# All products of an attention step in quarters of the TensorE array, with sums of 64 keys

## The chip, the cores and the metric

The kernel runs on one core of one Trainium2 chip. The metric is device time in microseconds, the median of several runs. Besides these runs one execution was taken by the hardware profiler; all rows of profiles here come from such an execution.

## The reference

A transformer block with modulated normalization over x of 32 batches x 256 tokens x 128 features, all in float32:

- `mod = silu(c) @ wmod` gives six rows for each batch; two of them are gates, kept at least 0.25 from zero.
- `h = layernorm(x) * (1 + ca) + sa`, then a root-mean-square norm of `h`, then queries, keys and values of 16 heads with 64 features each.
- `scores = q k^T`, without a scale, -inf where the key is later than the query. The softmax runs over the *query* axis (`axis=-2`): each key's column is normalized over the queries that see it.
- `z = attn @ v`, projected by `W_o`; `x = x + ga * (...)`.
- A second normalization and a mixture of 32 experts (4 groups of 8, two groups and six experts for a token, 64 inner features), with a shared expert and one anchor expert of a token: `x = x + gb * (routed + shared + 0.1 * anchor)`.

## The kernel before, in words

The tokens are cut into 16 chunks of 512 tokens (two batches). Attention takes 8 steps for a chunk, one for each pair of heads, so there are 128 steps; a step `s` belongs to chunk `s // 8`. What a step does is written out in the loop over `s`, and each engine runs its instructions in the order in which this loop issues them. No planner moves them.

In step `s` TensorE computes the scores of the pair `s`, the weighted sums of the pair `s - 2`, the queries and keys of the pair `s + 2`, the output product of the pair `s - 3`, and a quarter of the values of half a chunk. Keys stand on the partitions, since the softmax runs over queries.

- `score_products` (L528, products at L542) uses 64x64 quarters of the array: 64 keys of one head against the queries that see them, four at a time, into four banks of PSUM, one for each batch and head. `e` of a batch and head is a tile of 384 columns: 256 for the first 128 keys and 128 for the others.
- `lowest` (L566) on VectorE adds the mask and takes the minimum of each key's row; `exponential` (L576) on ScalarE takes the exponential and its sum. Queries carry a minus sign for this. `inverse_sums` (L584) and, on GpSimd, `scaled_values` (L595) scale the values by the inverse sums.
- `weighted_sums` (L613) multiplies 128 keys at a time: scaled values as weights of 128 rows and 64 columns, against 256 or 128 queries. `heads_out` (L624) copies the result to SBUF.
- Query, key, value and output products (`in_halves`, L492) run as two column halves of 128 rows by 64 columns. Their results leave PSUM by VectorE (values L504, queries L514) and ScalarE (keys L524). The products take turns on two banks of `ps_mm`; the sums have a bank of their own, the outputs another.

Around the steps lies work of whole chunks, cut into portions. A table gives each portion a step, counted from the chunk's first, and a place in that step (TOP, PROD, MID or END): loads of x and of modulation rows (`load_x`, `load_mod1`, `load_mods`), the first normalization of chunks to come, mostly on GpSimd, the gate and the sum of the attention's output (`rest_gate`, `rest_sum`), the second normalization, and the router with the sending of token rows to lists of experts. Each normalized chunk is turned through DRAM: `through_dram` (L422) writes it and reads it back in four blocked loads, all on SyncE's queue, and VectorE transposes 32x32 blocks (`norm1_turn`, `norm2_turn`). SyncE's queue holds nearly all loads and stores, in program order: 69 writes of blank rows too, three a step from step 0, and the weights of the expert stage, all of them in step 9 (`late_loads`). A buffer that is used again makes its DMA wait: `mb2`, loaded by `load_mods` in step 7 of a chunk, has one buffer, which `norm2_modulate` (L406, on GpSimd) of the chunk before frees.

After the 128 steps and a short run-out comes the expert stage over lists of 512 rows; the change touches only the names of its PSUM banks.

## Time and profile before

| | |
|---|---|
| median of 3 runs | 1357.53 us (1355.21 to 1361.33) |
| the profiled execution | 1363.71 us |
| span of its instructions | 1361.6 us |
| granted TensorE clock, mean | 0.988 |
| TensorE busy | 1309.9 us, 96% of the span |
| VectorE busy | 1035.6 us, 76% |
| ScalarE busy | 866.4 us, 64% |
| GpSimd busy | 759.4 us, 56% |

A span runs from the program's first instruction to its last. PE is TensorE's matmuls and PEld its weight loads, DVE VectorE, ACT ScalarE, POOL GpSimd, SP SyncE; SPq, POOLq are their queues. L613 is line 613 of the kernel. A float32 matmul appears as two passes, so a product of two halves counts four times. In a row with a bar, busy time and the mean of one instruction stand ahead of the idle time of the engine just before such instructions and what ended it. In a timeline the columns are the start and the length in microseconds, the engine, the line, the operation, output and inputs, and the count; in a list of waits they are the total, the number and the longest.

### The profile page before, as it was taken

How to read it: one execution, taken by the hardware profiler on the slowest of the kernel's cores; microseconds unless marked ns; L12 is line 12 of the kernel's file. 1: busy time of each engine (PE TensorE's matmuls, PEld its weight loads, DVE VectorE, ACT ScalarE, POOL GpSimd, SP SyncE). 2: the span in 40 equal slices, each digit the busy share in tenths (PEclk: the TensorE clock that was granted, in tenths of full speed). 3: DMA queues.
4: the chain of work that ended last, by engine and by line, in shares of the span. 5: the costliest groups of instructions: out<-in, count | busy, mean ns of one | idle time of the engine just before them, and what ended most of it. 6: DMA issues, size and time to landing. Idle time of an engine off the chain costs nothing. (4 is left out here: it accounts for less than half of the span.)

```text
span 1361.6 us, 37937 instructions
## 1 busy us (share of the span) xinstructions
PE 1309.9 (96%) x12491; PEld 812.7 (60%) x12491; DVE 1035.6 (76%) x4270; ACT 866.4 (64%) x2883; POOL 759.4 (56%) x1291
## 2 busy tenths in 40 slices
PE   6999899999999999999999997999999999999996
PEld 2555566666666666566566665466666666666664
DVE  5656688888888889889889776666855557888776
ACT  3868687778778777777777876444444544445451
POOL 2636368678669669669669557445332324434342
PEclk8999999999999999999999999999999999999998
DMA  5765821321321221221221212665555556777752
GB/s 159 232 203 200 275 62 32 77 65 37 78 66 40 68 66 40 68 66 40 68 66 40 52 42 55 148 152 130 147 139 127 140 145 183 191 190 191 197 166 70
DMA packets 270702, 153.58 MB, mean 113 GB/s; under 512 B 171014, under 2 KB 234759, under 8 KB 270508
## 3 DMA queue, kind: packets, MB, share of 16 engines
q1 hardware_dynamic: 258908, 129.70, 37.0%
q0 software_dynamic: 10624, 20.40, 4.3%
q8 instruction: 101, 1.65, 0.5%
q10 hardware_dynamic: 976, 1.06, 0.3%
q14 instruction: 93, 0.76, 0.2%
HBM read 91.27 MB, written 60.61 MB: 112 GB/s over the span
## 5 line engine op out<-in xcount | busy, mean ns | idle before, releaser
L576 ACT ACTIVATE e<-e,mn 128x256 f32<-128x256 f32 (+1 forms) x1024 | 453.0, 445 | 186.5 <-DVE mn L566 185.7
L566 DVE CUSTOM_DVE_ANT_0 e<-psc,mask 128x256 f32<-128x256 f32 (+1 forms) x1024 | 305.3, 344 | 7.4 <-ACT th L701 5.1
L1307 POOL DMA_INDIRECT y_d<-y,iy x140 | 140.5, 1003 | 283.1 <-ACT y L1304 247.0
L595 POOL TENSOR_TENSOR vs<-v,rc 128x256 f32<-128x256 f32 x256 | 151.6, 614 | 206.2 <-DVE rc L584 177.0
L1273 DVE TENSOR_TENSOR a<-a,pu 128x512 f32<-128x512 f32 (+2 forms) x185 | 121.5, 657 | 132.6 <-PE pu L1268 126.4
L542 PEld LDWEIGHTS psc<-q,k 64*64 64x64 f32 x4096 | 144.6, 133 | 108.2 <-issue 102.0
L1272 ACT ACTIVATE a<-pg 128x512 f32<-128x512 f32 (+2 forms) x185 | 106.2, 574 | 159.9 <-PE pg L1268 157.1
L613 PE MATMUL pav<-e,vs 128*64 128x256 f32 (+1 forms) x2048 | 195.2, 333 | 6.5 <-POOL vs L595 6.5
L576 ACT ACTIVATION_READ_ACCUMULATOR e<-e,mn 128x1 f32 x1024 | 192.9, 188 | 0.0
L1296 PEld LDWEIGHTS py<-wd_sb,a 128*128 128x128 f32 x1120 | 148.1, 193 | 70.1 <-issue 52.6
L1268 PE MATMUL pg<-h,wg 128*128 128x512 f32 (+2 forms) x370 | 182.5, 575 | 0.0
L1268 PE MATMUL pu<-h,wu 128*128 128x512 f32 (+2 forms) x370 | 181.9, 574 | 0.0
L542 PE MATMUL psc<-q,k 64*64 64x256 f32 (+3 forms) x4096 | 168.7, 303 | 0.0
L492 PEld LDWEIGHTS po<-wo_sb,z 128*64 128x64 f32 x2048 | 123.0, 140 | 70.9 <-issue 67.1
L613 PEld LDWEIGHTS pav<-e,vs 128*64 128x64 f32 x2048 | 127.1, 137 | 53.3 <-POOL vs L595 7.1
L881 POOL DMA_INDIRECT rows_d<-rows,ix x128 | 133.9, 1046 | 39.4 <-issue 33.9
L1296 PE MATMUL py<-wd_sb,a 128*128 x1120 | 150.8, 277 | 2.2 <-DVE a L1274 2.1
L492 PE MATMUL pk<-n_t,wqkv_sb 128*64 128x512 f32 x512 | 133.5, 600 | 3.1 <-DVE v L504 3.1
L492 PE MATMUL pv<-wqkv_sb,n_t 128*64 128x512 f32 x512 | 134.0, 604 | 2.2 <-DVE q L514 2.0
L492 PE MATMUL po<-wo_sb,z 128*64 128x128 f32 x2048 | 136.0, 276 | 0.0
L492 PE MATMUL pq<-n_t,wqkv_sb 128*64 128x512 f32 x512 | 133.6, 600 | 0.7 <-ACT n_t L326 0.7
L504 DVE TENSOR_TENSOR v<-pv,bv_sb 128x512 f32<-128x512 f32 x128 | 87.6, 684 | 58.2 <-PE pv L492 57.5
(240 smaller groups left out, 1798.7 us busy)
## 6 DMA issues: line engine op xcount, KB each, us to landing
rows_d<-blank SPq DMA_DIRECT2D x69, 366.0 KB
bt<-cd SPq DMA_DIRECT2D x70, 256.0 KB
rh<-rows_d SPq DMA_DIRECT2D x140, 64.0 KB
wgr<-in_w_gate_dram SPq DMA_DIRECT2D x35, 256.0 KB
wur<-in_w_up_dram SPq DMA_DIRECT2D x35, 256.0 KB
mb<-mod_dram SPq DMA_DIRECT2D x31, 256.0 KB
hb_ln<-hd_ln SPq DMA_DIRECT2D x124, 64.0 KB
s<-y_d SPq DMA_DIRECT2D x30, 256.0 KB
```

The costliest lines, as they stand in the source:

```text
L492: nc.tensor.matmul(ps[to], a[:, r], b, start=start, stop=stop)
L542: nc.tensor.matmul(pb[h][half * DH : (half + 1) * DH, n // 2 * P + n * DH : n // 2 * P + S,], k[r, o + n * DH : o + (n + 1) * DH], q[r, o ...
L566: nc.vector.tensor_tensor_reduce(e[:, cols], ps[:, cols], mask[:, cols], 1.0, 3e38, ALU.add, ALU.min, mn[:, b, kb, h : h + 1],)
L576: nc.scalar.activation(e[:, cols], e[:, cols], AF.Exp, bias=mn[:, b, kb, h : h + 1], scale=-1.0, accum_out=sm[:, b, kb, h : h + 1],)
L595: nc.gpsimd.tensor_tensor(vs[:, 2 * b : 2 * b + 2], vt[:, 2 * b : 2 * b + 2, col : col + P].rearrange("p k (h d) -> p k h d", h=2), rc[:, ...
L613: nc.tensor.matmul(pav[h * DH : (h + 1) * DH, o + kb * P : o + S], vs[:, 2 * b + kb, h, :], e[:, 0 : 2 * P] if kb == 0 else e[:, 2 * P : 3 ...
L881: sent = nc.gpsimd.indirect_dma_start(out=rows_d[:, :], out_offset=bass.IndirectOffsetOnAxis(ap=ix[:, k, i : i + 1], axis=0), in_=rows[:, ...
L1268: nc.tensor.matmul(ps[:, cols], t[key][k], t["h"][:, cols], start=True, stop=True)
L1272: nc.scalar.activation(a[:, cols], pg[:, cols], AF.Silu)
L1273: nc.vector.tensor_mul(a[:, cols], a[:, cols], pu[:, cols])
L1296: nc.tensor.matmul(t["py"][:, i, :], a[:, i * P : (i + 1) * P], w, start=k == 0 and i == part.start, stop=k == KU and i == part.stop - 1,)
L1307: sent = nc.gpsimd.indirect_dma_start(out=y_d[:, :], out_offset=bass.IndirectOffsetOnAxis(ap=ix[:, i : i + 1], axis=0), in_=y[:, i, :], in ...
```

## The change

All products of steps 3 to 123 are made as 64x64 quarters of the array (`step_in_quarters`). A product that adds 128 rows becomes two row halves, each of two column halves. The two row halves of one product add to the same bank, so they don't run at once: beside the first half of one product runs the second half of another, on another bank. Where a second half could reach a bank while the first is still adding, `done` puts a semaphore instruction into SyncE's queue that waits for the first, and the second waits for that; there are six of these in a step.

The weighted sums are made of 64 keys at a time, against the queries that see any of them (256, 192, 128, 64 columns, from the same tiles `e`).

A step's order on TensorE becomes: scores; first row half of some sums beside the second half of the values of the step before and one output block; queries, first half, beside three output blocks; keys, first half, beside the other sums; queries, second half, beside output blocks, first half; keys, second half, beside values, first half; then, in two steps of a chunk, the router's products (a new place LAST), each row half into a bank of its own, added by VectorE at TOP of the next step.

The sums' own bank goes; sums, queries, keys and values take turns on three banks. Evictions are issued later than their products: keys at the top of the next step, values after the next step's first reductions, queries after the step's last ones. Portions of the table move from TOP to PROD. The way through DRAM is split into a write and, one step later, the loads (`norm1_back`, `norm2_back`). The late weights are loaded one a step from step 17.

```diff
-        ps_mm = actx.enter_context(tc.tile_pool(name="ps_mm", bufs=2, space=PSUM))
-        ps_av = actx.enter_context(tc.tile_pool(name="ps_av", bufs=1, space=PSUM))
+        ps_mm = actx.enter_context(tc.tile_pool(name="ps_mm", bufs=1, space=PSUM))
         ps_wo = actx.enter_context(tc.tile_pool(name="ps_wo", bufs=1, space=PSUM))
+        turns_mm = [0]
+        bank_of = {}
+        def mm_bank(name):
+            turns_mm[0] += 1
+            bank_of[name] = f"mm{turns_mm[0] % 3}"
+            return ps_mm.tile([P, CH], F32, tag=bank_of[name], name=name)
...
-        def through_dram(src, tag, name):
+        def to_dram(src, name):
             hd = hdp.tile([CH, D], F32, tag="hd", name=f"hd_{name}")
             nc.sync.dma_start(out=hd.rearrange("(i p) d -> p i d", p=P), in_=src)
+            return hd
+        def from_dram(hd, tag, name):
             hb = ln.tile([P, CH // BLK, BLK], F32, tag=tag, name=f"hb_{name}")
             load_blocks(hb, hd)
             return hb.rearrange("p x r -> p (x r)")
...
+        def part_of(n):
+            return slice(n * DH, (n + 1) * DH)
+        def wait_for(made, first):
+            tc.add_manual_dep(
+                made.ins, first.ins.name,
+                mybir.DependencyInfo(mybir.DependencyClass.Sync, mybir.DependencyReason.DATA),
+                reason="both halves of the rows add to one bank",
+            )
+        def done(made):
+            seen = nc.sync.nop()
+            wait_for(seen, made)
+            return seen
+        def quarters(ps, r, a, b, start, stop, exchanged=False, behind=None):
+            for h in range(2):
+                made = nc.tensor.matmul(
+                    ps[part_of(1 - h if exchanged else h)], a[part_of(r), part_of(h)],
+                    b[part_of(r)], start=start, stop=stop,
+                )
+                if h == 0 and behind is not None:
+                    wait_for(made, behind)
+            return made
+        def sums_of_quarter(s, pav, b, n, start, stop, behind=None):
+            r = (0, 1, 1, 0)[n]
+            at = n // 2 * P + n * DH
+            for h in range(2):
+                made = nc.tensor.matmul(
+                    pav[part_of(h), b * S + n * DH : (b + 1) * S],
+                    step_of["vs", s][part_of(r), 2 * b + n // 2, h, :],
+                    step_of["e", s][b][h][part_of(r), at : n // 2 * P + S],
+                    start=start, stop=stop,
+                )
+                if h == 0 and behind is not None:
+                    wait_for(made, behind)
+            return made
+        def step_in_quarters(s):
+            w, o = s - LAG, s - LAG - 1
+            c, t = divmod(s + 2, NP)
+            co, to = divmod(o, NP)
+            h2, i = s // HALF + 1, s % HALF
+            cv, j = divmod(h2, 2)
+            n = chunk[c]["n"]
+            nv = chunk[cv]["n"][:, i * P : (i + 1) * P]
+            if i == 0:
+                step_of["v", h2] = vp.tile([P, NT, CH], F32, tag="vt", name=f"v_{cv}_{j}")
+            z = step_of.pop(("z", o))
+            qw, kw = (wqkv_sb[:, k, t * P : (t + 1) * P] for k in range(2))
+            vw = wqkv_sb[:, 2, j * CH : (j + 1) * CH]
+            def output_part(r, k, behind=None):
+                return quarters(
+                    chunk[co]["po"][:, k, :], r, z[:, k * P : (k + 1) * P], wo_sb[:, to, :],
+                    start=to == 0 and r == 1 and k == 0,
+                    stop=to == NP - 1 and r == 0 and k == NT - 1, behind=behind,
+                )
+            if to == 0:
+                chunk[co]["po"] = ps_wo.tile([P, NT, D], F32, tag="po", name=f"po_{co}")
+            pav = mm_bank(f"pav_{s}")
+            sums_of_quarter(w, pav, 0, 0, True, False)
+            rest_of_values()
+            sums_of_quarter(w, pav, 0, 3, False, False)
+            sums_of_quarter(w, pav, 1, 0, False, False)
+            output_part(1, 0, behind=later.pop("po", None))
+            sums = done(sums_of_quarter(w, pav, 1, 3, False, False))
+            pq = mm_bank(f"pq_{s}")
+            queries = quarters(pq, 0, qw, n, True, False)
+            for x in range(1, NT):
+                made = output_part(1, x)
+            step_of["pav", w] = pav
+            sums_of_quarter(w, pav, 0, 1, False, False, behind=sums)
+            pk = mm_bank(f"pk_{s}")
+            before_ = done(queries), done(made)
+            keys = done(quarters(pk, 0, kw, n, True, False))
+            sums_of_quarter(w, pav, 0, 2, False, False)
+            sums_of_quarter(w, pav, 1, 1, False, False)
+            sums_of_quarter(w, pav, 1, 2, False, True)
+            step_of.pop(("vs", w)), step_of.pop(("e", w))
+            heads_out(w)
+            quarters(pq, 1, qw, n, False, True, behind=before_[0])
+            for x in range(NT):
+                made = output_part(0, x, behind=None if x else before_[1])
+            later["po"] = done(made)
+            q, k = (qk.tile([P, CH], F32, tag=x, name=f"{x}_{s + 2}") for x in "qk")
+            step_of["q", s + 2], step_of["k", s + 2] = q, k
+            later["q"] = lambda: nc.vector.tensor_scalar(
+                q, pq, -1.0, negbq[:, t : t + 1], ALU.mult, ALU.add
+            )
+            quarters(pk, 1, kw, n, False, True, behind=keys)
+            later["k"] = lambda: nc.scalar.activation(
+                k, pk, AF.Identity, bias=bqk_sb[:, 1, t : t + 1]
+            )
+            pv = mm_bank(f"pv_{s}")
+            values_ = done(quarters(pv, 0, nv, vw, True, False, exchanged=i % 2 == 1))
+            def rest():
+                quarters(pv, 1, nv, vw, False, True, exchanged=i % 2 == 1, behind=values_)
+                later["v"] = lambda: nc.vector.tensor_add(
+                    step_of["v", h2][:, i, :], pv, bv_sb[:, j * CH : (j + 1) * CH]
+                )
+            later["pv"] = rest
+        later = {}
+        def rest_of_values():
+            later.pop("pv", lambda: None)()
+        def evict(name):
+            later.pop(name, lambda: None)()
...
-            chunk[c]["hb2"] = through_dram(chunk[c]["rows"][:, :, 0:D], "xhln2", f"ln2_{c}")
+            chunk[c]["hd2"] = to_dram(chunk[c]["rows"][:, :, 0:D], f"ln2_{c}")
+        def norm2_back(c):
+            chunk[c]["hb2"] = from_dram(chunk[c].pop("hd2"), "xhln2", f"ln2_{c}")
...
+        def spares(columns):
+            return [score_banks[1][r][:, 3 * P : 3 * P + columns] for r in range(2)]
+        def logits_in_quarters(c):
+            h2 = h2_all[c]
+            pl = spares(NT * E)
+            for i in range(NT):
+                for r in range(2):
+                    quarters(
+                        pl[r][:, i * E : (i + 1) * E], r, h2[:, i * P : (i + 1) * P], gw_sb,
+                        True, True,
+                    )
+            chunk[c]["pl"] = pl
+        def both(out_, ps):
+            nc.vector.tensor_copy(out_, ps[0])
+            nc.vector.tensor_add(out_, out_, ps[1])
+        def logits_tanh(c):
+            x, th = t_([NT, E], "lg", c), t_([NT, E], "th", c)
+            both(x.rearrange("p i e -> p (i e)"), chunk[c].pop("pl"))
+            nc.scalar.activation(th, x, AF.Tanh, scale=0.5)
             chunk[c]["th"] = th
...
-        TOP, PROD, MID, END = range(4)
-        NORM1 = 11
+        TOP, PROD, MID, END, LAST = range(5)
+        NORM1 = 12
         table = [
             (-15, END, load_x),
             (-15, END, load_mod1),
@@ -909,31 +1092,33 @@
             (-9, END, lambda c: norm1_squares(c, 1)),
             (-8, END, norm1_scale),
             (-7, END, norm1_send),
+            (-6, END, norm1_back),
             (-4, TOP, norm1_turn),
             (7, END, load_mods),
             (9, END, rest_bias),
             (11, TOP, rest_gate),
             (12, MID, rest_sum),
             (13, MID, norm2_moments),
-            (14, TOP, norm2_aggregate),
+            (14, PROD, norm2_aggregate),
             (14, END, norm2_normalize),
             (15, END, norm2_modulate),
             (16, END, norm2_send),
-            (19, TOP, norm2_turn),
+            (17, END, norm2_back),
+            (19, PROD, norm2_turn),
             (19, PROD, route_logits),
             (20, MID, route_sigmoid),
-            (21, TOP, route_pairs),
+            (21, PROD, route_pairs),
             (21, MID, lambda c: route_merge(c, 2)),
             (22, MID, lambda c: route_merge(c, 1)),
             (22, END, route_groups),
-            (23, TOP, route_mask),
+            (23, PROD, route_mask),
             (23, END, route_counts),
             (23, MID, route_top),
-            (24, TOP, lambda c: route_marks(c, 6)),
+            (24, PROD, lambda c: route_marks(c, 6)),
             (24, PROD, route_ranks),
             (24, MID, lambda c: route_marks(c, 1)),
-            (25, TOP, route_weights),
-            (26, TOP, route_place),
+            (25, PROD, route_weights),
+            (26, PROD, route_place),
             (26, END, route_write),
             *(
...
+        QUARTERS = range(LAG + 1, NS - HALF)
+        in_quarters = {
+            route_logits: ((19, LAST, logits_in_quarters), (20, TOP, logits_tanh)),
+            route_ranks: ((24, LAST, ranks_in_quarters), (25, TOP, ranks_sum)),
+        }
+        def portions_of(c):
+            for at, where, portion in table[0 if c else NORM1 :]:
+                if portion in in_quarters and c * NP + at in QUARTERS:
+                    yield from in_quarters[portion]
+                else:
+                    yield at, where, portion
...
+        late = late_loads()
         for s in range(NS + LAG + 1):
-            if s == NP + 1:
-                late_loads()
+            if s > 2 * NP:
+                next(late, None)
             ahead = s + 2 < NS
             deal(s, TOP)
+            evict("k")
             if s < NS:
                 score_products(s)
                 for h in range(2):
@@ -1130,6 +1331,24 @@
             if 1 <= s <= NS:
                 inverse_sums(s - 1)
                 scaled_values(s - 1)
+            if s in QUARTERS:
+                step_in_quarters(s)
+                evict("v")
+                deal(s, PROD)
+                for h in range(2):
+                    lowest(s, 1, h)
+                    exponential(s, 1, h)
+                evict("q")
+                if s + 1 not in QUARTERS:
+                    rest_of_values()
+                    evict("v")
+                deal(s, MID)
+                deal(s, END)
+                deal(s, LAST)
+                for i in blanks[s * 3 : s * 3 + 3]:
+                    write_blank(i)
+                step_of.pop("spare", None)
+                continue
```

## The prediction

> **What bounds the kernel now.** I read the page's busy shares first, then busy time by stage, then TensorE's timeline over one step, then the waits of the SyncE queue, then GpSimd's timeline over one chunk.
>
> ```profile
> PE 1309.9 (96%) x12491; PEld 812.7 (60%) x12491; DVE 1035.6 (76%) x4270; ACT 866.4 (64%) x2883; POOL 759.4 (56%) x1291
> ```
>
> ```profile
> 43.30:178.49 135.19, 127.34 (x1539) 77.55 (x1537) 88.24 (x440) 96.89 (x375) 61.24 (x112) 0.97 0.67 222
> 178.49:815.37 636.88, 633.00 (x7991) 391.29 (x7989) 542.67 (x2915) 491.50 (x1947) 462.56 (x857) 1.00 0.22 57
> 403.08:452.95 49.87, 49.87 (x634) 30.97 (x632) 42.92 (x229) 38.85 (x156) 37.74 (x69) 1.00 0.21 54
> ```
>
> The columns are stretch, length, busy PE, weight loads, VectorE, ScalarE, GpSimd, clock, DMA share, GB/s. The first stretch is steps 3 to 22, the second steps 23 to 123: together the 121 steps that the change rewrites, 772.1 us of the span. The third is one chunk of eight steps. In it TensorE has no idle time at a full clock, so TensorE bounds it; but VectorE is busy for 42.9 of 49.9 us, and GpSimd for 37.7. These are next in line.
>
> ```profile
> 399.53 1.03 PE L492 MATMUL pq<-n_t,wqkv_sb 128*64 128x512 f32 x4
> 400.39 1.03 PE L492 MATMUL pk<-n_t,wqkv_sb 128*64 128x512 f32 x4
> 401.25 1.04 PE L492 MATMUL po<-wo_sb,z 128*64 128x128 f32 x16
> 402.12 1.03 PE L492 MATMUL pv<-wqkv_sb,n_t 128*64 128x512 f32 x4
> 403.08 1.32 PE L542 MATMUL psc<-q,k 64*64 64x256 f32 x32
> 404.32 1.52 PE L613 MATMUL pav<-e,vs 128*64 128x256 f32 x16
> 405.68 0.61 PE L492 MATMUL psc<-gw_sb,h 128*64 128x32 f32 x16
> ```
>
> From start to start: 0.86 + 0.86 + 0.87 + 0.96 + 1.24 + 1.36 = 6.15 us a step. Each 512-column product takes 0.86 us for its two passes, 1.67 ns a column, whether it runs as two column halves or not. The scores are the only quarters now: 640 columns in each quarter of the array, 1.07 us at that rate, 1.24 measured. The weighted sums stream 768 columns a half, 1.28 us, 1.36 measured.
>
> **The change, part by part.** *Quarters.* A query, key, value or output product has the same work per quarter as before (2048 columns for the four, 3.41 us). It gains only what goes with the change of array form: pv takes 0.96 where pq takes 0.86, so 0.10 is lost on entering the scores, and about as much again on leaving them. *Sums of 64 keys* stream 256+192+128+64 = 640 columns per head and batch, half of them in each row half: 640 columns a quarter for both batches, 1.07 us for 1.36. Each quarter then streams 640+2048 columns, 4.48 us, beside 1.07 to 1.14 for the scores: 5.55 at least, and I take 5.65, with 0.1 for uneven ends. Against 6.15 that is 0.5 us, in 121 steps 60 us, if nothing else binds.
>
> A rule speaks against this. A step goes from 76 matmul passes to 120. The Trainium skill, "TensorE: Matmul & The Clock Gate", Part 1, says that with hardware decode off the sequencer spends about 62 ns on every matmul; by that (an estimate) 120 passes need 7.4 us, 1.3 us a step more than now, +150 us. The row decides: 32 score passes start within 1.24 us, 39 ns each, and that is their streaming. By the row, 120 passes in 5.65 us (47 ns) fit. I take no charge.
>
> *The order kept by SyncE.* The second row half of a bank waits for the first through a SyncE semaphore instruction, six a step. The trace of before has no such pair of hops. Near rows: the DMA that waits for `rows` starts 0.03 us after GpSimd ends; GpSimd starts 0.16 us after the reciprocal. So a hand-over costs 0.1 to 0.4 us. The slack is 384 columns (0.64 us) for the sums and 512 (0.85 us) for queries and keys, so it costs nothing where SyncE is free. Below nothing it cannot go. But SyncE stops being free-running: a DMA in its queue that waits now holds the hand-overs behind it, and TensorE behind these.
>
> ```profile
> SPq L432 <- POOL rows L406: 448.6, 15, 32.0
> SPq L432 <- DVE o_t L655: 74.1, 13, 10.4
> ```
>
> ```profile
> 407.27 1.18 POOL L595 TENSOR_TENSOR vs<-v,rc 128x256 f32<-128x256 f32 x2 [5.11 <-PE pq L492]
> ...
> 433.09 1.18 POOL L595 TENSOR_TENSOR vs<-v,rc 128x256 f32<-128x256 f32 x2
> ...
> 436.75 1.43 POOL L406 TENSOR_TENSOR rows<-ln_xh,mb 128x256 f32<-128x256 f32 x2
> ```
>
> ```profile
> 438.21 0.36 SPq L432 DMA_DIRECT2D mb<-mod_dram  x1
> 438.61 0.47 SPq L425 DMA_DIRECT2D hd_ln<-rows  x1
> 443.31 1.92 SPq L415 DMA_DIRECT2D hb_ln<-hd_ln  x4
> 445.34 0.43 SPq L425 DMA_DIRECT2D hd_ln<-ln_xh  x1
> 448.13 2.63 SPq L415 DMA_DIRECT2D hb_ln<-hd_ln  x4
> 450.86 0.43 SPq L442 DMA_DIRECT2D xt<-in_x_dram  x1
> 451.34 0.51 SPq L432 DMA_DIRECT2D mb<-mod_dram  x1
> ```
>
> SyncE spends 448.6 us, 30 us a chunk, waiting in `load_mods` for the buffer that `norm2_modulate` of the chunk before frees, harmlessly. After the change that DMA stands at END of step 7 (of each eight, counted from 0) behind that step's hand-overs and ahead of step 0's. When does GpSimd free it? Its work from step 3 to there has no gap: it starts with `vs` at 407.27, as soon as the reciprocal of 407.1 is out, and ends at 438.18: 31.1 us that the change doesn't touch. With T the start of the scores of step 3 (403.08), the reciprocal came at T+4.0. In the new order less of VectorE's work precedes it (`norm2_turn` goes behind): the query eviction of step 2 ends about T, the moments take 0.87, `rest_gate` 0.71, two score reductions 1.1 (0.55 a bank), the reciprocal 0.2: T+3.0. So the buffer is free at T+34.1, the DMA is issued by T+34.5, and the sums' hand-over of step 0 reaches TensorE at T+34.6.
>
> TensorE without waits would ask for it 5 x 5.65 + 0.45 (router logits, 405.68 to 406.11) + 2.85 = T+31.5: the wait costs 3.1 us, unless VectorE has made TensorE late already (below). From there step 0 has 1664 columns left, 2.8 us, 0.2 for ends and 0.2 for the ranks; then step 1, 5.65. At its END SyncE issues two round trips and two loads, 1.92+0.43+0.43+0.51 and gaps, 3.5 us, some 3.7 into step 2, whose hand-over is wanted at 2.85: 0.9 lost. Step 2 is 5.65+0.9. Sum: 34.6+3.2+0.3 (the ranks' two reads on VectorE, before the next scores may use their banks)+5.65+6.55 = 50.3 us a chunk, against 636.88 us for 12.6 chunks, 50.45, before. The 60 us are given back here.
>
> *Banks and evictions.* Three banks turn over four products: keys use the bank of the values before, which VectorE must have emptied 3.06 us into the step. Scores of the first batch are there at 0.8, reductions 1.1, reciprocal 0.2, `v` 0.68 (87.6 us for 128): 2.8. So 0.16 us of slack, and between the query eviction's end and the next reductions there are 0.85 us for MID, END and the next TOP. More than 1.0 us there makes TensorE wait. Boundaries from the groups' means: 2 to 3 (moments, gate) 1.6, loses 0.6; 3 to 4 (aggregate, logits, turn) 0.2 after the logits' own time; 5 to 6 (moments, merge) 1.8, loses 0.8; 6 to 7 (merge, groups) 1.75, loses 0.75. That is 2.3 us from step 3 to 0, inside the 3.1 us of the wait for GpSimd; without that cover they would count.
>
> *Steps 3 to 22.* Here SyncE ran ahead: 18 blank writes of 366 KB in one go, and the loads behind them came late.
>
> ```profile
> DVE ln_stats L379 <- DMA xt<-in_x_dram: 6.4, 1, 6.4
> ```
>
> Two steps took 11.5 and 12.4 us so, 11.7 over the usual. Held to three blanks a step (1.1 MB in 5.65 us, 195 GB/s, where the page's slices reach 275), that backlog shouldn't form. 20 x 5.65 + 0.45 + about 2.5 for VectorE + 5 for SyncE (steps 10, 16, 18, 19: the DMA issues above plus three blanks at 0.45 each) = 121, for 135.2: 14 less. The late weight loads, now one a step at 0.6 us, add 1.5 to stalls in steps 26 to 40. The expert stage keeps its work.
>
> **Sum.** 121 + 12.6 x 50.3 + 1.5 = 757.5 for 772.1: the profiled 1361.6 span becomes 1347, its execution of 1363.7 becomes 1349. The median of the runs, 1357.5, lies 6 below that execution: 1343.
>
> **Rivals.** *TensorE sets the pace* after all: GpSimd starts sooner (reciprocal at T+2.1, with no lateness) and evictions stay in their slack. Then a chunk is 34.6-0.9+15.2 = 48.9 and the time 1343-12.6x1.4 = 1325. For it: the free 0.5 us a step. Against: VectorE's 42.9 us leave 2.3 of slack in 45.2.
> *VectorE binds and it gets slower*: the place is the value eviction ahead of the key product. Adding its 42.9, about 0.6 for the new reads, and waits for scores and queries that the fixed order imposes, 52 us a chunk gives 1343+12.6x1.7 = 1364; it passes the old time once each chunk loses 1.2 us more than I count, that is if the boundaries lose 4.5 instead of 2.3 and the two key steps 0 and 1 half a us each.
> *The change doesn't do it*: row halves take turns. Each step then takes 1.1 + 2 x 4.5 = 10 us, +470 us. The scores, whose 16 products on four quarters finish in 1.24 us, speak against it.
>
> **How the numbers follow.** The likeliest, SyncE held by GpSimd, 0.50, at 1343, by itself 1331 to 1354 (a chunk 49.4 to 50.9, and the 14 us of the early steps between 10 and 16). TensorE's pace 0.22, 1322 to 1331. VectorE 0.25, 1352 to 1370. No overlap 0.03. Half a per cent, 6.8 us, is about what this kernel's runs tell from no change. Faster (below 1350.7): 0.22 and three quarters of 0.50, 0.59. Within: an eighth of 0.5 and most of VectorE's lower half, 0.20. Slower 0.21. The range that leaves 2 in 10: 1323 to 1368.
>
> **What would show it.** Right: in steps 24 to 123 a chunk of 50 us with TensorE idle 2 to 4 us, in step 0 of eight ahead of the row-half-1 sums, ended by SyncE, while SyncE's own wait is for `rows`; sums of 64 keys near 1.1 us; no step over 9 us before 178. Wrong: chunks of 46 (hand-overs and banks free), or stalls at the key product in most steps (VectorE), or 512-column quarter products starting one after the other on the two row halves.

## The result: 5.6% slower, and where the time went

The changed kernel takes 1434.42 us (median of four runs, 1426.57 to 1437.55) against 1356.53 us (now also of four runs, 1355.21 to 1361.33): a ratio of 1.056, with an interval of 1.051 to 1.061. I had predicted 1343 us. Its profiled execution took 1433.27 us, with a span of 1431.3.

The busy shares of the changed kernel, from the page:

```profile
PE 1316.2 (92%) x18143; PEld 985.9 (69%) x18143; DVE 1109.5 (78%) x4324; ACT 877.9 (61%) x2870; POOL 759.6 (53%) x1291
```

TensorE fell from 96% to 92% of a longer span, and VectorE gained 74 us of busy time, although the change gives it only a few small reads more. The stages next, with the same columns as before: steps 3 to 22, steps 23 to 123, and then the steps 1, 2 and 6 of one chunk (counted from its first step, 0).

```profile
42.43:179.33 136.90, 123.80 (x2431) 104.05 (x2433) 88.66 (x439) 96.75 (x376) 61.79 (x112) 0.96 0.58 201
179.33:883.78 704.45, 643.50 (x12750) 537.12 (x12743) 616.06 (x2971) 503.04 (x1932) 462.73 (x856) 0.98 0.21 56
...
534.82:540.70 5.88, 5.88 (x135) 5.26 (x130) 5.16 (x26) 4.05 (x16) 4.86 (x10) 1.00 0.16 47
540.70:547.76 7.06, 6.22 (x125) 4.83 (x121) 6.13 (x31) 5.20 (x23) 2.07 (x5) 1.00 0.64 150
566.45:576.94 10.49, 7.50 (x126) 6.23 (x122) 8.51 (x32) 5.24 (x21) 7.57 (x12) 0.84 0.09 29
```

Steps 3 to 22 lost 1.7 us instead of gaining 14; steps 23 to 123 lost 67.6 us. There are steps without any stall (5.88 us, TensorE busy all through) beside steps of 7 and 10 us in the same chunk. Over the twelve chunks of steps 24 to 119 the mean lengths, worked out from the starts of the scores, are:

| step of a chunk | 0 | 1 | 2 | 3 | 4 | 5 | 6 | 7 | sum, us |
|---|---|---|---|---|---|---|---|---|---|
| before | 6.42 | 6.16 | 6.21 | 6.96 | 6.15 | 6.15 | 6.15 | 6.25 | 50.4 |
| changed | 7.17 | 5.96 | 8.21 | 6.88 | 6.16 | 5.94 | 9.53 | 6.12 | 56.0 |

So 5.5 us a chunk are lost, in steps 0, 2 and above all 6. TensorE in the undisturbed step 1, the first rows of each section of the timeline:

```profile
534.82 0.41 PE L555 MATMUL psc<-q,k 64*64 64x256 f32 x1
...
535.94 0.38 PE L685 MATMUL pav<-e,vs 64*64 64x256 f32 x1
...
537.04 0.59 PE L672 MATMUL pq<-n_t,wqkv_sb 64*64 64x512 f32 x1
...
538.05 0.64 PE L672 MATMUL pk<-n_t,wqkv_sb 64*64 64x512 f32 x1
...
538.98 0.60 PE L672 MATMUL pq<-n_t,wqkv_sb 64*64 64x512 f32 x2
...
539.84 0.60 PE L672 MATMUL pk<-n_t,wqkv_sb 64*64 64x512 f32 x2
539.94 0.65 PE L672 MATMUL pv<-wqkv_sb,n_t 64*64 64x512 f32 x2
...
540.70 0.75 PE L555 MATMUL psc<-q,k 64*64 64x256 f32 x13
```

From start to start: 1.12 for the scores, 1.10 for the first half of the sums with the rest of the values, 1.01 for queries beside output blocks, 0.93 for keys beside sums, 0.86 and 0.86 for the second halves. That is 5.88, where I had 5.65.

The waits of steps 23 to 123 (total, number, longest), first those of GpSimd and TensorE, then the wait of SyncE's queue that I had put on the critical path:

```profile
POOL vs L608 <- DVE rc L597: 94.0, 37, 7.0
...
PE pk L672 <- DVE v L761: 39.5, 28, 3.0
...
PE pav L685 <- SPq L665: 20.2, 15, 2.9
```

```profile
SPq L442 <- POOL rows L413: 16.6, 13, 1.4
```

The wait of 448.6 us for `rows` is down to 16.6, and holds nothing up: in no step 0 does TensorE wait for a hand-over. GpSimd, which I had thought late, waits 94 us for VectorE's reciprocals. TensorE waits in two places: the key product for the value eviction (39.5 us; the slower rival's place), and the sums for a hand-over of SyncE (20.2 us).

**Step 6.** The timeline of that step, the rows of VectorE, GpSimd and the key product:

```profile
566.03 0.74 DVE L749 TENSOR_SCALAR q<-pq,negbq 128x512 f32<-128x512 f32 x1
...
566.70 0.80 DVE L888 TENSOR_TENSOR hi<-hi 128x32 f32<-128x32 f32 x1
...
567.34 2.80 POOL L413 TENSOR_TENSOR ln_xh<-ln_xh,mb 128x256 f32<-128x256 f32 x4
...
567.41 0.76 DVE L889 TENSOR_TENSOR mid<-hi 128x32 f32<-128x32 f32 x1
...
568.10 2.10 DVE L890 TENSOR_TENSOR lo<-lo 128x32 f32<-128x32 f32 x1
...
570.35 0.86 DVE L386 BATCH_NORM_STATS2 ln_stats<-x 128x6 f32<-128x128 f32 x4
...
572.34 0.64 DVE L761 TENSOR_TENSOR v<-pv,bv_sb 128x512 f32<-128x512 f32 x1
...
573.04 1.12 PE L672 MATMUL pk<-n_t,wqkv_sb 64*64 64x512 f32 x2 [3.00 <-DVE v L761]
```

Three operations of the router's merge, on 32 columns, take 0.80, 0.76 and 2.10 us. The second ends when the first of GpSimd's four modulation operations ends (568.17 and 568.10), the third when the last one does (570.20 and 570.14). Behind them on VectorE stand the moments, the reductions, the reciprocal and the value eviction; TensorE stands 3.0 us. The key product then runs at half speed (1.12 for 0.60 us): the granted clock of this step is 0.84. In five of these twelve chunks it was 0.75 to 0.84, and step 6 took 10.3 to 11.6 us; in six others it took 9.13. In the last one, where no modulation comes, it took 5.93.

**Step 2.** SyncE's queue, then the sums that wait for it:

```profile
429.39 1.92 SPq L422 DMA_DIRECT2D hb_ln<-hd_ln  x4
431.42 0.42 SPq L432 DMA_DIRECT2D hd_ln<-ln_xh  x1
431.94 2.51 SPq L452 DMA_DIRECT2D xt<-in_x_dram  x1
434.51 0.50 SPq L442 DMA_DIRECT2D mb<-mod_dram  x1
```

```profile
435.11 0.38 PE L685 MATMUL pav<-e,vs 64*64 64x192 f32 x2 [2.85 <-SPq L665]
```

The hand-over stands behind the DMA issues in program order; the last issue ends at 435.01, the sums start at 435.11. So the hand-over itself takes 0.1 us here once SyncE comes to it; the rest of TensorE's wait of 2.85 us is SyncE's time in DMA issues.

### The profile page after: what moved, and what is told of

Read it like the earlier page. It is cut to its first block, busy times and chain, and to the rows that moved or that the text cites. A ratio compares the mean times of both kernels' runs of the same rounds, so it can differ in the third digit from the quotient of the medians.

```text
span 1431.3 us, 50064 instructions
## 1 busy us (share of the span) xinstructions
PE 1316.2 (92%) x18143; PEld 985.9 (69%) x18143; DVE 1109.5 (78%) x4324; ACT 877.9 (61%) x2870; POOL 759.6 (53%) x1291
## 5 line engine op out<-in xcount | busy, mean ns | idle before, releaser
L685 PE MATMUL pav<-e,vs 64*64 64x256 f32 (+3 forms) x3872 | 328.8, 302 | 33.2 <-SPq L665 33.0
L672 PE MATMUL pk<-n_t,wqkv_sb 64*64 64x512 f32 x968 | 265.2, 622 | 39.8 <-DVE v L761 39.8
L685 PEld LDWEIGHTS pav<-e,vs 64*64 64x64 f32 x3872 | 243.5, 135 | 77.4 <-SPq L665 45.2
L672 PE MATMUL po<-wo_sb,z 64*64 64x128 f32 x3872 | 265.6, 276 | 0.6 <-DVE o_t L791 0.6
L672 PE MATMUL pq<-n_t,wqkv_sb 64*64 64x512 f32 x968 | 265.5, 608 | 0.0
L672 PE MATMUL pv<-wqkv_sb,n_t 64*64 64x512 f32 x968 | 260.8, 616 | 0.1
L672 PEld LDWEIGHTS po<-wo_sb,z 64*64 64x64 f32 x3872 | 228.4, 135 | 1.0 <-PE pv L672 1.0
L555 PEld LDWEIGHTS psc<-q,k 64*64 64x64 f32 x4096 | 190.1, 134 | 43.6 <-issue 25.1
L637 ACT COPY z<-pav 128x512 f32<-128x512 f32 x128 | 74.8, 585 | 171.9 <-PE pav L685 95.7
L749 DVE TENSOR_SCALAR q<-pq,negbq 128x512 f32<-128x512 f32 x121 | 90.5, 748 | 91.2 <-PE pq L672 72.0
```

The lines of the kernel that those rows point to most:

```text
L555: nc.tensor.matmul(pb[h][half * DH : (half + 1) * DH, n // 2 * P + n * DH : n // 2 * P + S,], k[r, o + n * DH : o + (n + 1) * DH], q[r, o ...
L672: made = nc.tensor.matmul(ps[part_of(1 - h if exchanged else h)], a[part_of(r), part_of(h)], b[part_of(r)], start=start, stop=stop,)
L685: made = nc.tensor.matmul(pav[part_of(h), b * S + n * DH : (b + 1) * S], step_of["vs", s][part_of(r), 2 * b + n // 2, h, :], step_of["e", ...
L749: later["q"] = lambda: nc.vector.tensor_scalar(q, pq, -1.0, negbq[:, t : t + 1], ALU.mult, ALU.add)
```

## The experiments

Each ratio is to the kernel before in the same set of runs, on one chip. The sets ran on several chips, which differ: the kernel before took 1365 us in the first set, 1388 to 1392 in the next three, 1356 in the last. The third and the fourth set ran on the same chip, and only the third has the changed kernel itself; in the first two sets the step lengths of the variants are set beside those of the changed kernel's first profile.

**First set: one cause each.** The modulation left out:

```diff
-            modulated(chunk[c]["h"], chunk[c]["h"], chunk[c].pop("mb"))
+            mb = chunk[c].pop("mb")
+            if c < 2:
+                modulated(chunk[c]["h"], chunk[c]["h"], mb)
```

> The changed kernel without the four modulation operations of the first normalization on GpSimd (4 x 0.70 us a chunk, left out from the third chunk on); all of VectorE's work stays where it is. Theory 'blocked' (GpSimd's tensor operations hold VectorE's two-input operations off): the merge operation that took 2.1 us in the sixth step of eight falls to about 0.2, the wait of the key product for the value eviction there from 3.0 to about 1, so the step goes from 9.1 to 11.5 us down to 7.0 to 7.5; over 12.6 chunks 25 to 40 us less, 1395 to 1410. Theory 'order' (VectorE's own work ahead of the value eviction is simply too long): that step stays above 8.5, and the time within 10 us of 1434.

1394.62 us, a ratio of 1.020 (1.015 to 1.024), 3.6 points less than the 1.056 of the changed kernel's first runs. The same merge operations in this run, with GpSimd's indirect transfer beside them:

```profile
547.47 0.97 POOL L1066 DMA_INDIRECT rows_d<-rows,ix  x1 [0.30 <-issue]
547.80 0.17 DVE L890 TENSOR_TENSOR hi<-hi 128x32 f32<-128x32 f32 x1
...
548.00 0.17 DVE L892 TENSOR_TENSOR lo<-lo 128x32 f32<-128x32 f32 x1
```

0.17 us each. Step 6 falls from 9.53 to 6.04, further than I expected (7.0 to 7.5), because all three merge operations had been held off, not one. 'Order' alone falls: from the first merge operation to the next reductions VectorE takes 1.3 us here, and step 6 is within 0.16 us of an undisturbed one.

The loads apart:

```diff
-            (-15, END, load_x),
-            (-15, END, load_mod1),
+            (-17, END, load_x),
+            (-17, END, load_mod1),
...
+            (8, END, load_mod2),    # mb2, taken out of load_mods
```

> The changed kernel with the loads of x and of the first modulation rows two steps earlier, and the load of mb2 one step later, so that SyncE has two DMAs less between the steps 1 and 2 of eight. Theory 'queue' (hand-overs behind SyncE's DMA issues): step 2 goes from 7.05 us to 6.0 to 6.5, the waits of the sums for SyncE (20 us from 180 to 884) to under 8, and the time falls by 10 to 25 us, to 1410 to 1425. Theory 'VectorE alone': no more than 5 us.

1414.07 us, 1.034 (1.030 to 1.038). Step 2 falls from 8.21 to 6.36, and the waits of the sums for SyncE from 20.2 us to 4.5 (180 to 880 us); 'queue' holds. Step 3 grows by 0.25.

The portions behind the value eviction:

```diff
-            (22, END, route_groups),
+            (22, MID, route_groups),
...
                 evict("v")
+                if s - 1 in QUARTERS:
+                    deal(s - 1, MID)
                 deal(s, PROD)
...
-                deal(s, MID)
+                if s + 1 not in QUARTERS:
+                    deal(s, MID)
```

> The changed kernel with VectorE's MID portions (merges, moments, maxima, marks) one step later, behind the value eviction instead of ahead of the next step's first reductions. If the value eviction behind these portions is what TensorE waits for, the waits of the key product for it (39.5 us from 180 to 884) fall to under 8, steps 6 and 0 of eight go from 9.1 and 7.2 to 6.0 to 6.5 and 5.9, and the time falls to 1370 to 1395. If VectorE has too much work in any place, the wait turns up again at the scores, for the banks of the second batch, and the time stays above 1415.

1407.88 us, 1.031 (1.027 to 1.035). Between the two: the waits for the value eviction fall from 39.5 us to 1.0 and step 6 to 5.91, but the steps 0 and 7 grow to 7.86 and 7.42, where the maxima, marks and masks now stand together behind the value eviction and make the second batch's reductions late. The place is right, but VectorE has no room for all of this in the new place either.

No quarters at all:

```diff
-        QUARTERS = range(LAG + 1, NS - HALF)
+        QUARTERS = range(0)
```

> The changed kernel with no step in quarters: table, split round trips, three banks in turn and late weights as changed, products in column halves of 128 rows as before. If the quarters with their order bring the loss: within 10 us of the kernel before, 1350 to 1367. If the table, banks or loads bring it: above 1395.

1362.9 us, 0.999 (0.997 to 1.001). Table, banks, split round trips and late weights by themselves are not the cause; the quarters with the order that they ask for are. Without quarters these parts even gain in steps 3 to 22 (124.2 us for 135.2) and give it back later (step 3 at 7.75).

**Second set: what holds VectorE off, and all moves at once.** Memsets in place of the modulation:

```diff
+            else:
+                for i in range(5):
+                    nc.gpsimd.memset(mb, 0.0)
```

> The changed kernel where from the third chunk on the four modulation operations of the first normalization are replaced by five memsets of 128x512 into the modulation rows' own tile: GpSimd is as long busy at the same place (5 x about 0.55 us, worked out from 0.42 us for 128x384 and 0.77 us for 128x732 in the trace), but only writes. If it is GpSimd's reads that hold VectorE's two-input operations off (the Trainium skill, SBUF, Who interferes with whom), the merge operation of 2.1 us falls to 0.2 and the time is that of the run without modulation, a ratio of 1.01 to 1.03 to the kernel before. If any busy GpSimd does it, the operation stays above 1.5 us and the ratio above 1.045.

```profile
584.89 2.89 POOL L473 MEMSET mb<- 128x512 f32 x5
585.24 0.18 DVE L893 TENSOR_TENSOR hi<-hi 128x32 f32<-128x32 f32 x1
...
585.44 0.19 DVE L895 TENSOR_TENSOR lo<-lo 128x32 f32<-128x32 f32 x1
```

GpSimd is busy for 2.89 us at the same place, and VectorE's operations take 0.18 to 0.19 us. Step 6 takes 6.51 us. So it is not that GpSimd is busy; what the memsets lack is the reading of SBUF. The Trainium skill, "SBUF — State Buffer", Who interferes with whom, says this: a VectorE instruction with two SBUF inputs contends with a GpSimd instruction that reads SBUF, not with one that only writes; one has the port for its whole instruction and the other blocks. The trace agrees, and adds that the loser need not get its turn between GpSimd's operations of 0.70 us each: the third merge operation waited for three of them. Why the first took 0.80 us, though by the record it began 0.64 us before the modulation, stays open. The ratio, 1.054 (1.050 to 1.059), missed what I expected, since a new stall of this chip hid the gain: step 3 took 10.3 us. The third set has the control.

All four moves (the loads apart, mb2 in step 9, and):

```diff
-            (-14, MID, norm1_moments),
+            (-13, PROD, norm1_moments),
-            (15, END, norm2_modulate),
+            (16, PROD, norm2_modulate),
-            (21, MID, lambda c: route_merge(c, 2)),
+            (22, PROD, lambda c: route_merge(c, 2)),
```

> The changed kernel with everything kept in the computation and four moves: the loads of x and of the modulation rows as in the run with loads apart; the first merge of the router from the end of step 5 to behind the value eviction of step 6; the second modulation from the end of step 7 to behind the scaled values of step 0; the moments of the first normalization behind the value eviction of step 3. If the three causes (VectorE blocked by GpSimd, VectorE's order, hand-overs behind DMA issues) are all there is beyond TensorE's own 5.9 us, a chunk falls from 55.9 to 48.5 to 50 and the ratio to before from 1.056 to 0.985 to 1.005. If the stalls only move, a chunk stays above 52 and the ratio above 1.02.

1450.36 us, 1.042 (1.038 to 1.045): step 0 at 6.25, step 6 at 6.66, but step 3 at 10.0, so a chunk of 56.2, far above what I expected if the three causes were all. The router's products, 32 short passes at the end of step 3, and what GpSimd does meanwhile:

```profile
554.09 0.55 PE L672 MATMUL psc<-gw_sb,h 64*64 64x32 f32 x8
554.82 0.33 PE L672 MATMUL psc<-gw_sb,h 64*64 64x32 f32 x4 [0.18 <-issue]
555.58 0.28 PE L672 MATMUL psc<-gw_sb,h 64*64 64x32 f32 x2 [0.42 <-issue]
556.29 0.23 PE L672 MATMUL psc<-gw_sb,h 64*64 64x32 f32 x1 [0.43 <-issue]
```

```profile
552.74 0.97 POOL L1066 DMA_INDIRECT rows_d<-rows,ix  x1 [0.31 <-issue]
554.02 0.97 POOL L1066 DMA_INDIRECT rows_d<-rows,ix  x1 [0.30 <-issue]
555.30 0.97 POOL L1066 DMA_INDIRECT rows_d<-rows,ix  x1 [0.30 <-issue]
```

TensorE gets a few instructions every 0.7 us and waits for nothing that the profile names, while GpSimd issues four indirect row transfers in a row. In the first profile of the changed kernel the same products started within 0.70 us.

The same with quarters only from step 24 on, `QUARTERS = range(3 * NP, NS - HALF)`:

> The same, with quarters from step 24 on only. If in steps 3 to 22 the hand-overs behind the writes of blank rows cost what the halves do not (136.9 us in quarters, 124.2 in halves with the changed table), this is 9 to 14 us faster than the run before it. If the early time has another cause (the loads), no difference beyond 4 us.

1431.59 us, 1.029 (1.025 to 1.032): 18.8 us less, 15.6 of them in steps 3 to 22 (124.3 for 139.9). So quarters cost that much in the early steps; that it is the hand-overs is read from the waits below, not from this run. And the kernel before with the late weights as in the change:

> The kernel before with one part of the change alone: the late weights one a step from step 17 instead of all in step 9. If the 11 us that the changed table without quarters gained in steps 3 to 22 come from this, steps 3 to 22 take about 124 us and the time falls by 8 to 11 us, a ratio of 0.992 to 0.994. If they come from the split round trips or the moved portions, within 3 us of before.

1389.18 us, 0.998 (0.996 to 1.000). Steps 3 to 22 took 131.0 us; 2.8 us in all, so most of the early gain of the changed table (11 us in the first set) must come from its other parts. Which, was not tried.

**Third set: the control.** The changed kernel, the four moves once more, and then mb2 in step 10 with quarters from step 24:

> The changed kernel itself, on the same chip as the three others of this set, because the set before showed waits of TensorE for nothing that the profile names (13.9 us at the router's products, none in the first profile of the changed kernel). A ratio of 1.05 to 1.065 if the chip is like the first; if this chip too makes the router's products wait, step 3 of eight is near 10 us instead of 6.6 and the ratio is above 1.07.

> The kernel with the four moves once more, beside its control. If the waits at the router's products of the last set (step 3 at 10.0 us, step 4 at 7.3) belong to that chip: step 3 at 6.5 to 7.1, a chunk of 49 to 50.5 us and a ratio of 0.985 to 1.01. If they belong to this kernel: step 3 near 10 again, a chunk near 55, a ratio of 1.03 to 1.045.

> The four moves, quarters from step 24 on only, and the load of mb2 one step later again, which takes one of three DMA issues from between the steps 1 and 2. On a chip like the first: step 2 from 6.57 to about 6.1, steps 3 to 22 at 124, so 15 to 20 us below the kernel with the four moves, a ratio of 0.97 to 0.99: faster than before. If quarters can't win: 1.00 or above.

1499.81, 1447.13 and 1425.95 us: 1.078 (1.073 to 1.083), 1.041 (1.036 to 1.045) and 1.026 (1.021 to 1.030). The changed kernel's step 3 is at 10.2 here, against 6.88 in its first profile: the stall belongs to the chip, not to the moves. Its step 6 is at 9.71, so the 6.51 of the memsets is a fall here too. Against their control the moves take 52.7 us off, and the third kernel 73.9, a chunk from 60.3 to 55.3. But none is faster than before.

The modulation left out of the kernel before:

> The kernel before without the four modulation operations of the first normalization on GpSimd (left out from the third chunk on). In the changed kernel this gave 3.1 us a chunk and more. If that came from where VectorE's work stands ahead of the value eviction in the changed kernel, here it gives nothing: within 4 us of before. If GpSimd's operations slow the kernel before as well, 15 us or more.

1392.91 us, 1.001 (0.998 to 1.003): nothing. The same 2.8 us of GpSimd's work that cost the changed kernel 3.6 points cost the old order nothing.

**Fourth set: the transfers spread**, at most two in a step:

```diff
-                for n, at in enumerate((27, 27, 27, 27, 28, 29, 29, 30))
+                for n, at in enumerate((27, 27, 28, 28, 29, 29, 30, 30))
```

> The four moves, quarters from step 24 and mb2 later, and now at most two of the router's indirect row transfers on GpSimd in a step (two in each of steps 3 to 6 of eight) instead of four in step 3. On chips where TensorE waits in step 3 for nothing that the profile names, such gaps lie beside GpSimd's indirect transfers. If four in a row bring them: step 3 from 10.0 to below 7.5 there, a chunk of 49 to 52 us and a ratio below 1.00. If not: step 3 near 10, a ratio of 1.02 to 1.03. On a chip like the first, where there are none of these gaps: a ratio of 0.97 to 0.99.

> The changed kernel with only the sends spread. The blocked merges, the value evictions and the hand-overs stay. If four transfers in a row are what the chips differ in: step 3 at 6.6 to 7.5 on any chip, a ratio of 1.045 to 1.06. If not: step 3 near 10 on a chip like the last, a ratio near 1.078.

> The kernel before with only the sends spread. On a chip like the last (its step 4 of eight at 7.7 to 8.0 us instead of 6.15): faster by up to 20 us if four in a row bring this, a ratio of 0.985 to 0.995; on a chip like the first, within 4 us.

The last version with the moves, the changed kernel and the kernel before take 1405.85, 1439.94 and 1386.54 us: 1.013 (1.009 to 1.018), 1.037 (1.033 to 1.041), 1.000 (0.998 to 1.002). Step 3 falls to 7.85 and 7.63, and the changed kernel, unlike the one before, gains four points. The kernel with the moves stays above the one before, which I had expected it to beat: its steps 5 to 7 grow (6.46, 6.86, 7.30), so the transfers cost where they are.

The changed kernel gains in a second place, which I had not expected: step 6 falls from 9.71 to 6.93. The two transfers that stand ahead of the modulation in GpSimd's order now run later, the modulation starts 1.9 us into the step instead of 0.4, and the merges, from 0.02 to 0.4 us, are over by then (0.18 us each).

**Fifth set: no transfers** for the chunks 1 to 13 (`if 1 <= c < NCH - 2: return` in `route_send`), with zeros written to the expert results: the last version with the moves, the kernel before, and the changed kernel.

> The four moves, quarters from step 24, mb2 later, and the router's row transfers of the chunks 1 to 13 left out (the lists stay blank there; in their place 8 MB of zeros are written to the expert results before the loop, some 25 us at the start in all three kernels of this set). If the transfers bring both the gaps at the router's products and the late evictions of the sums: chunks of 48 to 49.5 us, against 49.9 in halves without transfers, so 5 to 25 us faster than the halves of this set. If quarters lose by themselves: chunks above 50.5.

> The kernel before with the same transfers left out and the same zeros written. Chunks of 49.3 to 49.9 us on any chip, since TensorE has no other waits; on a chip like the last three sets 1.3 to 2 us a chunk less than with the transfers.

> The changed kernel with the same transfers left out and the same zeros written. The blocked merges (at least the one beside the modulation), the value evictions and the hand-overs stay: chunks of 53 to 55 us, 40 to 65 us slower than the halves of this set, on any chip. If the transfers are the main cause after all: within 15 us of the halves.

1378.76 (1377.28 to 1381.45), 1387.38 (1381.95 to 1389.10) and 1423.61 us (1420.49 to 1430.32). Writing the zeros costs all three some 30 us at the start (step 3 begins at 72 to 74 us instead of 43), so they compare with each other only. Here are steps 23 to 123 of each, in this order:

```profile
198.52:829.37 630.85, 621.04 (x12699) 527.43 (x12697) 575.25 (x2966) 499.14 (x1926) 375.64 (x763) 1.00 0.19 45
```

```profile
204.73:839.86 635.13, 633.37 (x7990) 390.88 (x7988) 548.66 (x2915) 491.04 (x1947) 370.81 (x767) 1.00 0.18 44
```

```profile
211.31:880.33 669.02, 635.93 (x12751) 534.19 (x12743) 586.49 (x2971) 501.68 (x1932) 376.39 (x765) 0.99 0.19 46
```

TensorE idles for 9.8, 1.8 and 33.1 us of them; a chunk takes 49.9, 50.3 and 53.0.

*Quarters with the moves against halves:* 8.6 us less in all, 0.6%, at the lower end of what I expected, though both chunks are 0.4 us longer than the longest that I expected. But only 4.3 of this lies in steps 23 to 123. Steps 3 to 22, which run in halves in both kernels, give 6.6 (125.0 for 131.6), as the changed table without quarters had done in the first set, and the time after step 123 takes 2.7 back. So what quarters win when little disturbs them is 4.3 us here, from one profile of each, with the moved portions in it.

*The changed kernel* loses 36 us against halves, less than the 40 to 65 that I expected. On a chip where the kernel before took about as long (1356.53 us; 1355.69 in this set) it had lost 78 with its transfers. So, if the two chips are alike, more than half of the loss went with the transfers, although the first profile shows no gap at the router's products. It went in step 6, where I had expected the blocked merges to stay: from 9.53 to 6.68. The transfers of chunk 0 were still sent, in steps 27 to 30; step 30, the step 6 of that chunk, took 10.73 us, the ten after it 6.3 to 6.7. Step 30, then step 62, GpSimd's work and the third merge operation:

```profile
260.34 0.97 POOL L1068 DMA_INDIRECT rows_d<-rows,ix  x1 [0.30 <-issue]
261.31 2.78 POOL L415 TENSOR_TENSOR ln_xh<-ln_xh,mb 128x256 f32<-128x256 f32 x4
262.06 2.09 DVE L892 TENSOR_TENSOR lo<-lo 128x32 f32<-128x32 f32 x1
```

```profile
478.10 2.78 POOL L415 TENSOR_TENSOR ln_xh<-ln_xh,mb 128x256 f32<-128x256 f32 x4
480.95 0.18 DVE L892 TENSOR_TENSOR lo<-lo 128x32 f32<-128x32 f32 x1
```

With two transfers ahead of it the modulation starts 0.9 us into the step and lies on the merges. Without them it starts 2.1 us before the step, and is over when the third merge operation comes. So the stall of step 6 takes three things: the merges ahead of the value eviction, the modulation's reads, and the transfers that hold the modulation back until the merges run. What is left of the loss lies mostly in step 2 (8.22), step 0 (7.02) and steps 3 to 22 (139.5 for 131.6).

The gaps at the router's products are not settled by this set, for this chip doesn't have them: step 27, with transfers of chunk 0, took 7.11 us in the kernel with the moves and 7.66 in the changed one, step 35, without any, 7.01 and 7.76. In the third set the kernel with the same moves took 9.72 in step 27. What ties the gaps to the transfers is the fourth set.

## Why the prediction was wrong, step by step

**TensorE's step, 5.65 us: undersized.** Quarters overlap as assumed: the halves of `pk` and `pv` start 0.1 to 0.2 us apart on the two row halves, and the rival of no overlap is out. The scores took 1.12 us, where I gave them 1.07 to 1.14. But the step is 0.33 us over the least of 5.55, not 0.1: the sections of queries and keys alone take 1.94 for 1.71. So 5.88, and the gain at stake was 0.27 us a step (27 us over steps 23 to 123), not 0.5. The rule of 62 ns a pass would have made a step 7.4 us; 120 passes in 5.88 are 49 ns, so the row was the better guide.

**Hand-overs cost nothing where SyncE is free: right.** In step 1 TensorE doesn't wait; in step 2 the hop is 0.1 us. *Where SyncE is busy*, I gave step 2 a loss of 0.9 us; in the later chunks it was 1.1 to 1.4, in the earlier ones 1.6 to 5.6, 2.3 on the mean. In the chunk shown the load of x took 2.51 us to issue instead of 0.43, and a low clock followed (0.84 over the step). The mechanism was right; the issue time, taken from one chunk, was too small.

**The wait for GpSimd's buffer, my likeliest case: not there.** The buffer was to come free at T+34.1 and to be asked for at T+31.5. In the chunk shown (T = 547.76) the load is issued at 585.44, T+37.7, and step 0 starts at 583.16, with the hand-over wanted 2.85 us later, at T+38.2. VectorE had made TensorE later than GpSimd. I had named that as the condition of this case, and the condition failed.

**"Boundaries from the groups' means": the step that failed.** At the boundary from step 5 to 6 I counted 1.8 us. It was 4.4 (566.70 to 571.13); with the modulation left out it is 1.3. I took VectorE's operations at a fixed cost and gave no cost to what GpSimd does beside them. The means in the trace of before were already not the operations' own durations: there `mid<-hi` takes 0.16 us in some places and 0.65 in others. In the new timing three merge operations run beside the modulation, because two row transfers stand ahead of it on GpSimd. The slower rival named the place, the value eviction ahead of the key product, and its threshold, 1.2 us a chunk more than counted; this one boundary gave 2.6. The boundary from 7 to 0, which I had not counted, cost 0.9 us (step 0 at 7.17, and at 6.25 with the moves): two copies of 0.5 to 0.8 us beside the other modulation, 0.18 each with the moves. Without the first modulation the stall of step 6 is gone (a chunk of 52.3), without the transfers nearly so (53.0), and in the old order, which doesn't ask for the value eviction so soon, leaving it out gains nothing.

The sum of my first rival was wrong apart from this. It put 15.2 us behind the hand-over of step 0 where the terms above give 15.7, and still had GpSimd hold that step; a chunk at TensorE's own pace, by my terms, is the 46 us named among the signs, not 48.9.

**Steps 3 to 22: 121 predicted, 136.9 measured.** Most of these steps are undisturbed (5.7 to 6.3 us), as expected without a backlog of blanks. But a few stand behind SyncE's issues: step 3 took 10.9 us, step 11 7.8, step 19 8.5, and step 18 13.3. SyncE's rows in step 18, and what waits for them:

```profile
139.64 2.81 SPq L422 DMA_DIRECT2D hb_ln<-hd_ln  x4
142.56 0.43 SPq L432 DMA_DIRECT2D hd_ln<-ln_xh  x1
143.08 0.45 SPq L452 DMA_DIRECT2D xt<-in_x_dram  x1
143.59 0.54 SPq L442 DMA_DIRECT2D mb<-mod_dram  x1
144.17 1.49 SPq L227 DMA_DIRECT2D rows_d<-blank  x3
145.71 1.51 SPq L148 DMA_DIRECT2D wd_sb<-in_w_down_dram  x1
```

```profile
147.33 0.58 PE L685 MATMUL pav<-e,vs 64*64 64x192 f32 x2 [4.83 <-SPq L665]
```

These are seven and a half microseconds of issues ahead of a hand-over that was wanted by 142, and the granted clock of the step is 0.74. I had given SyncE 5 us for four such steps, and this one alone lost 7.4. With quarters from step 24 on these steps take 124.3.

**The clock** was in no term of the sum. Stalls of 2.5 to 3.0 us in step 6 were followed in five of eleven chunks by a granted clock of 0.75 to 0.84 over the step, 1.2 to 2.4 us more. The Trainium skill, "TensorE: Matmul & The Clock Gate", Part 1, has the clock fall back after at least one idle window of about 3.4 us, of a window that runs freely. By that, stalls of 3.0 us would cost nothing; here the measurement differs, and decides.

**Shown and open.** Shown, each by a run that takes it away: the operations blocked by the modulation, the transfers that bring it onto them, the value eviction's place, the hand-overs behind DMA issues. Open: why TensorE gets its instructions in bursts beside indirect transfers on some chips; whether the moves beat the kernel before, with its transfers, on a chip like the first, since those runs fell on the others; and what quarters win without the moved portions.

## What to carry to other kernels

When engines hand work over every few microseconds, the mean of a small VectorE operation is not a constant: look at what GpSimd does beside it and at what stands ahead of that in GpSimd's order, and count two-input operations at the length of the GpSimd burst that they may meet. A queue that has only issued DMAs becomes part of TensorE's path as soon as it carries hand-overs; move the DMA issues out of their way first. A gain that exists only with every engine on time (0.27 us in 6.15) needs slack in the others before it is worth its risk.

## What the hardware showed that I had not expected

A VectorE operation that takes 0.17 us alone took 2.10 beside three GpSimd operations in a row: it waited for the burst, not for one of them. The operation before it had come through after the first.

While GpSimd's indirect transfers run, a hand-over between two other engines takes longer. This is the median time from the end of the last sums to ScalarE's copy of them, where ScalarE was free, worked out from the rows of steps 23 to 123:

| | a transfer running | none running |
|---|---|---|
| changed kernel, first profile | 0.31 us | 0.20 us |
| changed kernel, third set's chip | 1.02 us | 0.15 us |
| four moves, second set's chip | 1.02 us | 0.14 us |

On the two slower chips TensorE's instructions came in bursts 0.7 us apart while four transfers ran; spreading the transfers took 2.2 and 2.6 us off step 3 on one of them. No run without transfers fell on such a chip. The old order lost there too (in its two variants of the second and third sets step 4 took 7.9 and 7.8 us for 6.15), but quarters lost more: a 5.6% loss on one chip was 7.8% on another.
